# A low-rank conditioned feed-forward kernel in float32: factored adapters on 32x32 TensorE tiles, other DMA shapes, and an order by half tiles

## The chip, the cores and the metric

The kernel runs on one core of a Trainium2 chip. The metric is device time in microseconds (us) of one execution. The engines are named as the profile names them: PE is TensorE (PEld its weight loads), DVE is VectorE, ACT is ScalarE, POOL is GpSimd, SP is SyncE, which only issues transfers. Sixteen DMA engines move data between DRAM and the on-chip memory of 128 partitions (SBUF); PSUM is the memory into which PE accumulates.

## The reference

All data are float32. There are 8 batches of 512 tokens, rows of 2048 features. `itok` names one of 32 adapters for each batch; R is 16 and there are 8 experts.

```python
# y: a dense layer with a low-rank adapter per batch
base_out = einsum('bti,oi->bto', x, W) + b
lora_h   = einsum('bti,bir->btr', x, lora_As[itok])
y        = base_out + einsum('btr,bro->bto', lora_h, lora_Bs[itok]) * 2.0
# top-1 routed low-rank experts on y
logits = einsum('bsd,ed->bse', y, route_w)
topk_v, topk_idx = top_k(logits, 1)
h   = einsum('bsd,erd->bser', y, A)
wh  = (one_hot(topk_idx) * topk_v)[..., None] * h
out = x + einsum('bser,eor->bso', wh, Bw) * 1.0
```

Only 136 projections of y are needed, 128 for h (8 experts x 16) and 8 for the logits. With P the 2048x136 matrix of both, y P = x (W^T P) + b P + 2 (x A_b)(B_b P), so y itself is never formed.

## The kernel before, in words

**Fold.** P comes as `pj`: 16 chunks of 128 rows by 136. For each of 16 blocks of 128 rows of W (`load_w`, L101, 1 MB each, four buffers), ACT reorders the block into `wv` (L82) and PE accumulates W^T P into PSUM with 16 products (L189, `fold_w`). The result is `c_sb`, 2048x136. Beside this PE forms the bias part (`fold_bias`, L204), turns the gathered rows of the second adapter matrix (`turn_adapters`, L220), and multiplies them with P (`project_adapters`, L227) into `gm`, masked by batch. The adapters' rows come by two indirect transfers of POOL (L155, L162).

**Adapters.** `fold_adapters(b)` (L264) multiplies A of a batch with its part of `gm` and adds `c_sb`: a full matrix `m` of 2048x136 for each batch (L274 PE, L282 DVE). It is called for two batches at a time, so four times, in the order of `units`: two units of 256 tokens of a batch b, then two of batch b+4.

**Tokens.** A unit of 256 tokens is two tiles of 128. `load_x` brings a unit as [128 partitions, 8 groups of 32 tokens, 512 features]: partition quarter i holds features 512 i to 512 i + 511, and each partition of it one of 32 tokens. Four transfers do this, one for each quarter, two on SP's queue and two on ACT's (L115). `turn_x` (L296) turns a tile in 32x32 blocks on DVE, `heads` (L302) runs 16 products with `m` (each a float32 product of two instructions, L307) and then routes on DVE (L312 to L323); `turn_heads` (L334, L336) turns the weighted heads; `delta` (L339) runs 4 products for a quarter of the features (L343), turns them back on DVE (L345) and adds them to x on POOL (L350); `store` (L356) writes the unit in four transfers, two on SP's queue and two on POOL's. There are five buffers of x.

**Order.** The program is written out by hand (`manual_schedule`), and each engine runs its instructions in the order of the text. A loop over n interleaves heads of unit n with deltas of unit n-1 and the turn of unit n+1; the load of unit n+3 follows the store of unit n-1.

The views that shape the transfers before are these:

```python
        nc.sync.dma_start(out=wt, in_=w[ts(oc, P), :])
...
        return dram[b, ts(k, U), :].rearrange("(g t) (i d) -> i t g d", t=Q, i=NQ)
...
        for i, eng in ((0, nc.sync), (2, nc.scalar), (1, nc.sync), (3, nc.scalar)):
            eng.dma_start(out=xt[ts(i, Q)], in_=src[i])
```

Of the kernel before, what the change touches and what calls it, by code (L numbers as in the profile page):

```python
# [14 lines left out]
COND_SCALING = 2.0  # L15
# [3 lines left out]
def kernel(  # L19
# [28 lines left out]

    nc = tc.nc
# [15 lines left out]
    TPU = U // P  # L65
    NG = U // Q
    GJ = 4
    PH = P // 2
    HB = B // 2
    assert B * R == P and ER == P  # L70

    const = ctx.enter_context(tc.tile_pool(name="const", bufs=1))
    cpool = ctx.enter_context(tc.tile_pool(name="cpool", bufs=6))
    rpool = ctx.enter_context(tc.tile_pool(name="rpool", bufs=4))
    xpool = ctx.enter_context(tc.tile_pool(name="xpool", bufs=5))
    dpool = ctx.enter_context(tc.tile_pool(name="dpool", bufs=2))
    small = ctx.enter_context(tc.tile_pool(name="small", bufs=2))
    ps_s = ctx.enter_context(tc.tile_pool(name="ps_s", bufs=2, space=bass.MemoryType.PSUM))

    def chunked(copy, dst, src):  # L80

        copy(  # L82
            dst.rearrange("p j (i a) -> p j i a", a=Q),
            src.rearrange("p (i j a) -> p j i a", i=NQ, a=Q),
        )
# [6 lines left out]
    pj = cpool.tile([P, NO, NP], F32, tag="c", name="pj")  # L92
    proj_v = proj.rearrange("(c p) e -> p c e", p=P)
    bias_sb = const.tile([P, NO], F32, name="bias_sb")
    fb = const.tile([P, NJ, P], F32, name="fb")
# [3 lines left out]
    def load_w(oc):  # L99
        wt = rpool.tile([P, D], F32, tag="r", name=f"w_{oc}")  # L100
        nc.sync.dma_start(out=wt, in_=w[ts(oc, P), :])  # L101
        w_tiles.append(wt)

    units = [UPB * (b + h * HB) + k for b in range(HB) for h in range(2) for k in range(UPB)]
    x_tiles = {}

    def rows_of(dram, u):
        b, k = divmod(u, UPB)
        return dram[b, ts(k, U), :].rearrange("(g t) (i d) -> i t g d", t=Q, i=NQ)

    def load_x(u):
        xt = xpool.tile([P, NG, DQ], F32, tag="x", name=f"x_{u}")
        src = rows_of(x, u)
        for i, eng in ((0, nc.sync), (2, nc.scalar), (1, nc.sync), (3, nc.scalar)):
            eng.dma_start(out=xt[ts(i, Q)], in_=src[i])  # L115
        x_tiles[u] = xt

    nc.scalar.dma_start(out=pj[:, :2], in_=proj_v[:, :2])
    load_w(0)
    nc.scalar.dma_start(out=pj[:, 2:], in_=proj_v[:, 2:])  # L120
    nc.scalar.dma_start(out=bias_sb, in_=bias)
    for oc in range(1, 4):
        load_w(oc)
# [3 lines left out]
    make_identity(nc, ident)  # L127

    own_i = const.tile([P, B], I32, name="own_i")
    nc.gpsimd.iota(own_i, pattern=[[-R, B]], base=0, channel_multiplier=1)  # L130
    own = const.tile([P, B], F32, name="own")
# [6 lines left out]

    rank_i = const.tile([P, E], I32, name="rank_i")
    nc.gpsimd.iota(rank_i, pattern=[[-1, E]], base=E, channel_multiplier=0)  # L140
    rank = const.tile([P, E], F32, name="rank")
    nc.vector.tensor_copy(rank, rank_i)


    it_f = const.tile([P, B], F32, name="it_f")
    nc.vector.tensor_scalar(it_f, it_i, float(R), None, ALU.mult)
    nc.vector.tensor_tensor(it_f, it_f, own, ALU.add)
    nc.vector.tensor_tensor(it_f, it_f, mask, ALU.mult)
    row_f = const.tile([P, 1], F32, name="row_f")
    nc.vector.tensor_reduce(row_f, it_f, AX.X, ALU.add)  # L150
    row_i = const.tile([P, 1], I32, name="row_i")
    nc.vector.tensor_copy(row_i, row_f)
    raw = [xpool.tile([P, 2, D], F32, tag="x", name=f"raw_{k}") for k in range(2)]
    ad_b = raw[0][:, 0, :]
    nc.gpsimd.indirect_dma_start(  # L155
        out=ad_b,
        out_offset=None,
        in_=cond_b,
        in_offset=bass.IndirectOffsetOnAxis(ap=row_i, axis=0),
    )  # L160
    ad_ar = raw[0][:, 1, :]
    nc.gpsimd.indirect_dma_start(  # L162
        out=ad_ar,
        out_offset=None,
        in_=cond_a,
        in_offset=bass.IndirectOffsetOnAxis(ap=row_i, axis=0),
    )
    ad_a = const.tile([P, NJ, P], F32, name="ad_a")
    chunked(nc.gpsimd.tensor_copy, ad_a, ad_ar)


    c_sb = cpool.tile([P, NJ, NP], F32, tag="c", name="c_sb")
    GRP = 512 // NP
    groups = [(j0, min(GRP, NJ - j0)) for j0 in range(0, NJ, GRP)]
    c0b = const.tile([P, NP], F32, name="c0b")
    gm = const.tile([P, B, NP], F32, name="gm")

    with tc.tile_pool(name="ps_c", bufs=len(groups), space=bass.MemoryType.PSUM) as ps_c:
# [4 lines left out]
        def fold_w(oc):  # L183
            wv = dpool.tile([P, NJ, P], F32, tag="d", name=f"wv_{oc}")
            chunked(nc.scalar.copy, wv, w_tiles[oc])
            for pc, (j0, n) in zip(pcs, groups):
                for k in range(n):

                    nc.tensor.matmul(  # L189
                        pc[:, k, :],  # L190
                        wv[:, j0 + k, :],
                        pj[:, oc, :],
                        start=(oc == 0 and k == 0),
                        stop=(oc == NO - 1),
                        skip_group_check=True,
                    )
                if oc == NO - 1:
                    nc.scalar.copy(c_sb[:, j0 : j0 + n, :], pc[:, :n, :])

        def fold_bias():  # L200

            pb = ps_s.tile([1, NP], F32, tag="s", name="pb")
            for oc in range(NO):
                nc.tensor.matmul(  # L204
                    pb,
                    bias_sb[:, oc : oc + 1],
                    pj[:, oc, :],
                    start=(oc == 0),
                    stop=(oc == NO - 1),
                )  # L210
            c0 = const.tile([1, NP], F32, name="c0")
            nc.vector.tensor_copy(c0, pb)  # L212
            nc.gpsimd.partition_broadcast(c0b, c0)  # L213

        ad_bT = raw[1][:, 1, :].rearrange("p (c q) -> p c q", q=P)

        def turn_adapters(g):
            pt = ps_s.tile([P, 4, P], F32, tag="s", name=f"pbT_{g}")
            for k in range(4):
                nc.tensor.transpose(pt[:, k, :], ad_b[:, ts(4 * g + k, P)], ident)  # L220
            nc.scalar.copy(ad_bT[:, 4 * g : 4 * g + 4, :], pt)

        def project_adapters():

            pg = ps_s.tile([P, NP], F32, tag="s", name="pg")
            for oc in range(NO):
                nc.tensor.matmul(  # L227
                    pg,
                    ad_bT[:, oc, :],
                    pj[:, oc, :],  # L230
                    start=(oc == 0),
                    stop=(oc == NO - 1),
                )
            g_sb = const.tile([P, NP], F32, name="g_sb")
            nc.vector.tensor_copy(g_sb, pg)  # L235
            for b in range(B):
                nc.vector.tensor_scalar(
                    gm[:, b, :], g_sb, mask[:, b : b + 1], COND_SCALING, ALU.mult, ALU.mult
                )

        for oc in range(NO):
            fold_w(oc)
            if oc + 4 < NO:
                load_w(oc + 4)
            if oc == 2:
                fbr = raw[1][:, 0, :]
                nc.scalar.dma_start(out=fbr, in_=ffn_b)
                chunked(nc.gpsimd.tensor_copy, fb, fbr)
            if oc in (3, 6, 9):
                load_x(units[oc // 3 - 1])  # L250
            if oc == 7:
                fold_bias()
            if oc in (8, 9, 10, 11):
                turn_adapters(oc - 8)
            if oc == 12:
                project_adapters()
                load_x(units[3])
    ps_m = ctx.enter_context(tc.tile_pool(name="ps_m", bufs=2, space=bass.MemoryType.PSUM))
# [3 lines left out]
    m_tiles = {}  # L262

    def fold_adapters(b):  # L264
        pair = (b, b + HB)
        for bb in pair:
            m_tiles[bb] = cpool.tile([P, NJ, NP], F32, tag="c", name=f"m_{bb}")
        for j0, n in groups:
            pms = [
                ps_m.tile([P, GRP, NP], F32, tag="m", name=f"pm_{bb}_{j0}") for bb in pair  # L270
            ]
            for k in range(n):
                for h, bb in enumerate(pair):
                    nc.tensor.matmul(  # L274
                        pms[h][:, k, :],
                        ad_a[ts(h, PH), j0 + k, :],
                        gm[ts(h, PH), bb, :],
                        start=True,
                        stop=True,
                    )  # L280
            for h, bb in enumerate(pair):
                nc.vector.tensor_tensor(  # L282
                    m_tiles[bb][:, j0 : j0 + n, :],
                    c_sb[:, j0 : j0 + n, :],
                    pms[h][:, :n, :],
                    ALU.add,
                )


    xT_tiles = {}  # L290
    wh_tiles = {}
    whT_tiles = {}

    def turn_x(u, t):
        xT = rpool.tile([P, NJ, P], F32, tag="r", name=f"xT_{u}_{t}")
        nc.vector.transpose(  # L296
            xT.rearrange("p j (g t) -> p g j t", t=Q),
            x_tiles[u][:, ts(t, NQ), :].rearrange("p g (j a) -> p g j a", a=Q),
        )
        xT_tiles[u, t] = xT  # L300

    def heads(u, t):  # L302
        xT = xT_tiles.pop((u, t))
        m = m_tiles[u // UPB]
        ph = ps_s.tile([P, NP], F32, tag="s", name=f"ph_{u}_{t}")
        for j in range(NJ):
# [127 lines left out]
```

## Time and profile before

| | |
|---|---|
| time, median of 3 runs | 440.67 us (436.3 to 443.87) |
| time of the profiled execution | 436.82 us |
| its span, first to last instruction | 435.0 us |
| mean granted clock of TensorE | 0.915 of full |
| read from and written to DRAM | 54.60 MB and 33.55 MB, 203 GB/s over the span |

The profile's page has six parts: busy time of each engine; the span in 40 slices (a digit is a tenth; PEclk is the clock granted to TensorE, DMA the mean busy share of 16 DMA engines, GB/s what they moved); the DMA queues with packets, MB and share; the chain of waits followed back from the last instruction; the costliest groups of instructions as "line engine operation, out<-in, shapes, xcount | busy us, mean ns | idle before, and what ended it"; and the transfers as "out<-in, queue, xcount, KB each, median us from issue to landing". The queue q1 is SP's, q10 ACT's, q0 POOL's. A separate answer gives the same quantities for chosen stretches of time, and another the chain piece by piece in order of time.

In order of time, the first matmul starts at 21.6 us, the fold of W ends at about 105, the first heads run from about 120, and the last store is issued at 422.

### The profile page before, as it was taken

Reading aid. Unit: us, or ns where it says so; the run is one execution under the profiler, and the core shown is the slowest. Engines: PE = TensorE matmul, PEld = TensorE weight load, DVE = VectorE, ACT = ScalarE, POOL = GpSimd, SP = SyncE. Lnnn points to the kernel's source line nnn. Section 1 sums busy time; section 2 is a strip of 40 time slices with the busy share of each in tenths; the row PEclk is TensorE's granted clock in tenths of the full one; section 3 lists DMA queues with packets and bytes.
Section 4 is the critical chain, followed back from the end, with each engine's and each line's share of the span. In section 5 each row is a group of like instructions: output and inputs, shape, how many; then the busy total and the mean of one; then the engine's idle time right before and its main releaser. Section 6 shows DMA issues by size and latency. Waiting matters only on the chain.

```text
span 435.0 us, 5824 instructions
## 1 busy us (share of the span) xinstructions
PE 358.9 (83%) x2416; PEld 332.2 (76%) x2416; DVE 228.3 (52%) x388; ACT 42.1 (10%) x43; POOL 176.4 (41%) x110
## 2 busy tenths in 40 slices
PE   0099987598788996999999699999969999999900
PEld 0099866598687995999889599999858998999800
DVE  1000000010557886388787628888863887886620
ACT  0335332434000000000000000000000000000000
POOL 2111000000001764067675505867550585768780
PEclk9999999999579996799999759999976999999975
DMA  8999999991004099937999994599999459995596
GB/s 258 400 322 277 252 296 284 266 305 53 0 1 98 2 203 240 267 62 154 227 293 286 237 269 85 129 231 292 283 233 294 87 128 226 299 202 121 129 196 152
DMA packets 35738, 88.54 MB, mean 204 GB/s; under 512 B 2560, under 2 KB 4608, under 8 KB 33280
## 3 DMA queue, kind: packets, MB, share of 16 engines
q1 hardware_dynamic: 19712, 50.34, 43.7%
q10 hardware_dynamic: 11072, 18.95, 18.7%
q0 software_dynamic: 4928, 18.88, 15.5%
q8 instruction: 19, 0.31, 0.3%
q14 instruction: 7, 0.06, 0.0%
HBM read 54.60 MB, written 33.55 MB: 203 GB/s over the span
## 4 chain that ended last, share of the span: by engine, by line
PE 56%; DMA 12%; DVE 10%; POOL 7%; ACT 3%; issue 3%; ACTq 1%; POOLq 0%; SPq 0%; DVEq 0%
PE ph L307 20%; PE pd L343 15%; PE pc L189 10%; DMA out_dram<-x 9%; PE pm L274 8%; POOL x L350 7%; DMA x<-in_x_dram 3%; DVE m L282 3%; ACT wv L82 3%; DVE xT L296 3%; DVE dl L345 2%; PE pb L204 1%; PE pg L227 1%; ACTq L115 1%; POOL out_dram L356 1%
## 5 line engine op out<-in xcount | busy, mean ns | idle before, releaser
L350 POOL TENSOR_TENSOR x<-x,dl 128x1024 f32<-128x1024 f32 x64 | 149.6, 2360 | 189.4 <-DVE dl L345 187.0
L307 PE MATMUL ph<-m,xT 128*128 128x136 f32 x1024 | 131.9, 290 | 2.7 <-DVE xT L296 2.7
L307 PEld LDWEIGHTS ph<-m,xT 128*128 128x128 f32 x1024 | 129.8, 200 | 4.5 <-DVE xT L296 3.0
L343 PE MATMUL pd<-whT,fb 128*128 128x256 f32 x512 | 116.2, 380 | 3.6 <-ACT whT L336 3.6
L343 PEld LDWEIGHTS pd<-whT,fb 128*128 128x128 f32 x512 | 94.9, 190 | 16.6 <-ACT whT L336 4.9
L345 DVE STREAM_TRANSPOSE dl<-pd 128x1024 f32<-128x1024 f32 x64 | 80.0, 1250 | 24.1 <-PE pd L343 13.5
L189 PE MATMUL pc<-pj,wv 128*128 128x136 f32 x512 | 63.9, 287 | 32.4 <-ACT wv L82 32.4
L189 PEld LDWEIGHTS pc<-pj,wv 128*128 128x128 f32 x512 | 62.4, 196 | 33.8 <-ACT wv L82 33.6
L296 DVE STREAM_TRANSPOSE xT<-x 128x2048 f32<-128x2048 f32 x32 | 72.7, 2273 | 0.0
L274 PE MATMUL pm<-gm,ad_a 64*128 64x136 f32 x256 | 43.1, 416 | 14.2 <-DVE m L282 13.6
L274 PEld LDWEIGHTS pm<-gm,ad_a 64*128 64x128 f32 x256 | 35.3, 280 | 21.5 <-DVE m L282 20.2
L282 DVE TENSOR_TENSOR m<-c_sb,pm 128x408 f32<-128x408 f32 (+1 forms) x48 | 23.6, 526 | 34.1 <-PE pm L274 34.1
L336 ACT COPY whT<-pw 128x256 f32<-128x256 f32 x16 | 6.0, 373 | 295.0 <-PE pw L334 162.9
L82 ACT COPY wv<-w 128x2048 f32<-128x2048 f32 x16 | 30.3, 1899 | 29.3 <-PE pc L189 11.1
L312 DVE TENSOR_TENSOR hl<-ph,c0b 128x136 f32<-128x136 f32 x32 | 9.6, 299 | 32.2 <-PE ph L307 32.2
L212 DVE COPY c<-pb 1x136 f32<-1x136 f32 x1 | 0.3, 287 | 49.6 <-PE pb L204 49.6
L356 POOL DMA_DIRECT2D out_dram<-x x32 | 18.8, 592 | 4.8 <-POOL x L350 4.8
L235 DVE COPY g_sb<-pg 128x136 f32<-128x136 f32 x1 | 0.3, 300 | 34.9 <-PE pg L227 34.9
L213 POOL PARTITION_BROADCAST c0b<-c x1 | 0.5, 475 | 24.6 <-DVE c L212 24.6
L323 DVE TENSOR_TENSOR wh<-hl,rw 128x128 f32<-128x128 f32 x32 | 9.4, 293 | 1.1
L321 DVE TENSOR_SCALAR rw<-rank,win,top 128x8 f32<-128x8 f32 x32 | 9.3, 291 | 1.2
L334 PE MATMUL pw<-ident,wh 128*128 128x128 f32 x32 | 6.3, 274 | 2.1 <-DVE wh L323 2.1
(38 smaller groups left out, 63.4 us busy)
## 6 DMA issues: line engine op xcount, KB each, us to landing
w<-in_w_dram SPq DMA_DIRECT2D x16, 1024.0 KB, 16.1
x<-in_x_dram ACTq DMA_DIRECT2D x32, 512.0 KB, 8.8
x<-in_x_dram SPq DMA_DIRECT2D x32, 512.0 KB, 15.9
out_dram<-x SPq DMA_DIRECT2D x32, 512.0 KB, 9.0
out_dram<-x POOLq DMA_DIRECT2D x32, 512.0 KB, 10.9
raw<-in_ffn_b_dram ACTq DMA_DIRECT2D x1, 1024.0 KB, 4.8
pj<-in_proj_dram ACTq DMA_DIRECT2D x1, 952.0 KB, 22.2
pj<-in_proj_dram ACTq DMA_DIRECT2D x1, 136.0 KB, 9.0
```

Source lines behind the costliest of these rows:

```text
L82: copy(dst.rearrange("p j (i a) -> p j i a", a=Q), src.rearrange("p (i j a) -> p j i a", i=NQ, a=Q),)
L189: nc.tensor.matmul(pc[:, k, :], wv[:, j0 + k, :], pj[:, oc, :], start=(oc == 0 and k == 0), stop=(oc == NO - 1), skip_group_check=True,)
L274: nc.tensor.matmul(pms[h][:, k, :], ad_a[ts(h, PH), j0 + k, :], gm[ts(h, PH), bb, :], start=True, stop=True,)
L282: nc.vector.tensor_tensor(m_tiles[bb][:, j0 : j0 + n, :], c_sb[:, j0 : j0 + n, :], pms[h][:, :n, :], ALU.add,)
L296: nc.vector.transpose(xT.rearrange("p j (g t) -> p g j t", t=Q), x_tiles[u][:, ts(t, NQ), :].rearrange("p g (j a) -> p g j a", a=Q),)
L307: nc.tensor.matmul(ph, xT[:, j, :], m[:, j, :], start=(j == 0), stop=(j == NJ - 1))
L312: nc.vector.tensor_tensor(hl, ph, c0b, ALU.add)
L323: nc.vector.tensor_tensor(wh.rearrange("p (e r) -> p e r", r=R), hl[:, :ER].rearrange("p (e r) -> p e r", r=R), rw.unsqueeze(2).to_broadca ...
L343: nc.tensor.matmul(pd[:, k, :], fb[:, j0 + k, :], whT_tiles[u], start=True, stop=True)
L345: nc.vector.transpose(dl.rearrange("p g (k a) -> p k g a", a=Q), pd.rearrange("p k (g t) -> p k g t", t=Q),)
L350: nc.gpsimd.tensor_tensor(xs, xs, dl, ALU.add)
L356: eng.dma_start(out=dst[i], in_=xt[ts(i, Q)])
```

## The change

Adapters: no matrix per batch is formed. `cm` holds the folded W once, 136 columns, with 16 columns on either side for the adapter matrix A of an even and of an odd batch. `heads` multiplies x with 152 of these columns, so that PE forms x A_b beside x W^T P. `turn_low` copies the 16 numbers of each token to SBUF and turns them in 32x32 blocks; `add_low` multiplies each quarter of 32 tokens, on a diagonal 32x32 tile of PE, with `g4`, which holds the small matrix of the batch and the bias on each quarter of partitions, and adds to the same PSUM sums. `spread_adapters` makes `g4`. ACT copies the next batch's A into `cm`.

Fold: W, proj and the adapters are laid out by features i, j, a (i a quarter of 512 features, j one of 16 chunks, a one of 32), so that DVE's block turns replace PE's transposes; the copies into `wv` are halved between ACT and DVE; the bias product moves to DVE; the gathers become eight.

Transfers: x and out move in eight transfers of a unit, one for each group of 32 tokens, over 128 partitions; W in 16 and proj in 16 transfers over 128 partitions, with the views below. All of these are issued by SP. The order of the units is that of the batches.

Order: a loop over half tiles writes for each step half of a tile's heads, one quarter of a delta, the turn of half a tile, and the previous quarter's turn back and add.

```diff
-        wt = rpool.tile([P, D], F32, tag="r", name=f"w_{oc}")
-        nc.sync.dma_start(out=wt, in_=w[ts(oc, P), :])
+    proj_v = proj.rearrange("(i j a) e -> j i a e", i=NQ, a=Q)
+    w_v = w.rearrange("(i j a) d -> j i a d", i=NQ, a=Q)
+    def load_pj(j):
+        nc.sync.dma_start(out=pj[:, j, :], in_=proj_v[j])
+        nc.sync.dma_start(out=wt, in_=w_v[j])
...
     def rows_of(dram, u):
         b, k = divmod(u, UPB)
-        return dram[b, ts(k, U), :].rearrange("(g t) (i d) -> i t g d", t=Q, i=NQ)
+        return dram[b, ts(k, U), :].rearrange("(g t) (i d) -> g i t d", t=Q, i=NQ)
     def load_x(u):
         xt = xpool.tile([P, NG, DQ], F32, tag="x", name=f"x_{u}")
         src = rows_of(x, u)
-        for i, eng in ((0, nc.sync), (2, nc.scalar), (1, nc.sync), (3, nc.scalar)):
-            eng.dma_start(out=xt[ts(i, Q)], in_=src[i])
+        for g in range(NG):
+            nc.sync.dma_start(out=xt[:, g, :], in_=src[g])
...
+        def gather(v, table):
+            for m in range(NQ):
+                nc.gpsimd.indirect_dma_start(
...
+        gather(ad_br, cond_b)
+        gather(ad_ar, cond_a)
+        nc.gpsimd.dma_start(out=bias_o, in_=bias)
+        nc.gpsimd.dma_start(out=fbr, in_=ffn_b)
...
-            chunked(nc.scalar.copy, wv, w_tiles[oc])
+            chunked(nc.scalar.copy, wv, w_tiles[oc], 0)
+            chunked(nc.vector.tensor_copy, wv, w_tiles[oc], 1)
...
+        def turn_bias():
+            for i in range(NQ):
+                for k in range(NQ):
+                    nc.gpsimd.tensor_copy(
...
+        def fold_bias(js):
+            for j in js:
...
+                    nc.vector.scalar_tensor_tensor(
+                        bp, pj[:, j, :], bias_q[:, j : j + 1], bp, ALU.mult, ALU.add
+                    )
...
+        def spread_adapters(b0):
+            n = min(GRP, B - b0)
+            pq = ps_s.tile([P, GRP, NP], F32, tag="s", name=f"pq_{b0}")
+            nc.tensor.matmul(
+                pq[:, :n, :],
+                sel.rearrange("p i s -> p (i s)"),
+                gm[:, b0 : b0 + n, :],
+                start=True,
+                stop=True,
+            )
+            nc.vector.tensor_tensor(
+                g4[:, b0 : b0 + n, :],
+                pq[:, :n, :],
+                c0q.unsqueeze(1).to_broadcast([P, n, NP]),
+                ALU.add,
+            )
...
-    def fold_adapters(b):
...
+        for j in range(h * HJ, (h + 1) * HJ):
             nc.tensor.matmul(
-                ph, xT[:, j, :], m[:, j, :], start=(j == 0), stop=(j == NJ - 1)
+                ph_tiles[t],
+                xT_tiles[t][:, j, :],
+                cm[:, j, ds(s * R, NA)],
+                start=(j == 0),
+                stop=(j == NJ - 1),
             )
+    def turn_low(t):
+        s = batch_of(t) % 2
+        nc.scalar.copy(hls[t % 2][:, :R], ph_tiles[t][:, ds(s * NP, R)])
+        hT = small.tile([P, Q], F32, tag="hT", name=f"hT_{t}")
+        nc.vector.transpose(hT, hls[t % 2])
+        hT_tiles[t] = hT
+    def add_low(t):
+        b = batch_of(t)
+        s = b % 2
+        hT = hT_tiles.pop(t)
+        for i in range(NQ):
+            nc.tensor.matmul(
+                ph_tiles[t][ts(i, Q), ds((1 - s) * R, NP)],
+                hT[ts(i, Q), :],
+                g4[ts(i, Q), b, :],
+                start=False,
+                stop=True,
+                skip_group_check=True,
+                tile_position=(i * Q, i * Q),
+            )
...
+    def add_delta(u, q):
...
+        nc.gpsimd.tensor_tensor(xs, xs, dl, ALU.add)
+        if q == NQ - 1:
+            xt = x_tiles.pop(u)
+            dst = rows_of(out, u)
+            for g in range(NG):
+                nc.sync.dma_start(out=dst[g], in_=xt[:, g, :])
+            if u + 5 < NU:
+                load_x(u + 5)
...
+    for n in range(2 * NT + 2 * TPU + 1):
+        t, h = divmod(n, 2)
+        if t < NT:
+            heads(t, h)
+        if h == 0 and 0 < t <= NT:
+            route(t - 1)
+        if piece(n - 1):
+            add_delta(*piece(n - 1))
+        turn_x(t + 1, h)
+        if piece(n):
+            delta(*piece(n))
+        if h == 0 and 0 < t <= NT:
+            turn_heads(t - 1)
+        if h == 1 and t < NT:
+            turn_low(t)
+            add_low(t)
+            b, k = divmod(t, TPU * UPB)
+            if k == 0 and 0 < b < B - 1:
+                nc.scalar.copy(
+                    cm[:, :, ds((b + 1) % 2 * NA, R)], ad_aT[:, :, ts(b + 1, R)]
+                )
```

## The prediction, made before the changed kernel was run

> **What bounds the kernel now.** I read the page's span and slices first, then the chain of waits, then the groups, then stretches of the DMA rows.
>
> ```profile
> span 435.0 us, 5824 instructions
> PE 358.9 (83%) x2416; PEld 332.2 (76%) x2416; DVE 228.3 (52%) x388; ACT 42.1 (10%) x43; POOL 176.4 (41%) x110
> DMA  8999999991004099937999994599999459995596
> GB/s 258 400 322 277 252 296 284 266 305 53 0 1 98 2 203 240 267 62 154 227 293 286 237 269 85 129 231 292 283 233 294 87 128 226 299 202 121 129 196 152
> PE 56%; DMA 12%; DVE 10%; POOL 7%; ACT 3%; issue 3%; ACTq 1%; POOLq 0%; SPq 0%; DVEq 0%
> ```
>
> TensorE sets the end for 56% of the span and the transfers for 12%, but the DMA digits are 9 in more than half of the slices: the transfers are nearly a second bound. The chain inside a batch, in order of time, shows the pace of TensorE:
>
> ```profile
> 260.24 3.45 PE pd L343 x16
> 263.70 3.71 PE ph L307 x32
> 267.40 3.45 PE pd L343 x16
> 271.07 3.71 PE ph L307 x32
> ```
>
> So a unit of 256 tokens costs 2 x (3.71 + 3.45) = 14.3 us of TensorE plus 0.4 us of small transposes. It moves 2.1 MB in and 2.1 MB out. At 435 us nothing else matters as long as the 88.5 MB move near 300 GB/s, so the question that I put to the change is: how many of the 16 DMA engines does each transfer run on, and how fast is one? The page answers the first for the kernel before.
>
> ```profile
> q1 hardware_dynamic: 19712, 50.34, 43.7%
> q10 hardware_dynamic: 11072, 18.95, 18.7%
> w<-in_w_dram SPq DMA_DIRECT2D x16, 1024.0 KB, 16.1
> x<-in_x_dram SPq DMA_DIRECT2D x32, 512.0 KB, 15.9
> out_dram<-x SPq DMA_DIRECT2D x32, 512.0 KB, 9.0
> ```
>
> Queue q1 is SP's. Its x and out rows are 64 x 256 rows of 2 KB = 16384 packets, its W rows 16 x 128 of 8 KB = 2048. 19712 - 18432 = 1280 = 80 transfers x 16: one closing packet for each engine that took part. So all 80 run on 16 engines (q10 gives the same: 10496 rows + 36 x 16 = 11072). The speed of one engine, from the table of stretches:
>
> ```profile
> core 0: us, PE busy (x) PEld busy (x) DVE busy (x) ACT busy (x) POOL busy (x), PEclk, DMA share, GB/s
> 8.00:20.00 12.00, 0.00 (x0) 0.00 (x0) 0.82 (x5) 1.62 (x2) 2.05 (x2) 1.00 1.02 416
> 136.00:138.00 2.00, 2.00 (x15) 1.90 (x14) 0.75 (x4) 0.00 (x0) 0.00 (x0) 1.00 1.01 204
> 162.00:164.00 2.00, 1.38 (x16) 0.93 (x14) 1.63 (x2) 0.00 (x0) 2.00 (x1) 1.00 1.04 283
> 423.00:427.00 4.00, 0.00 (x0) 0.00 (x0) 0.00 (x0) 0.00 (x0) 0.00 (x0) 0.50 0.93 189
> ```
>
> W alone, 128 partitions and 8 KB rows: 416/16 = 26 GB/s per engine. x loads alone, 32 partitions and 2 KB rows: 204/16/1.01 = 12.6. Stores alone: 189/16/0.93 = 12.7. Loads and stores mixed: 283/16/1.04 = 17. A 2 KB packet thus costs between 79 ns (at 26 GB/s) and 162 ns (at 12.6), and 120 ns when mixed. The trace does not say whether 162 comes from 2 KB or from 16 engines meeting in 32 partitions.
>
> **The change, transfers first.** The new views put a dimension of 4 outermost on the DRAM side: `g i t d` for x and out (i=4, t=32, 2 KB rows), `j i a d` for W and `j i a e` for proj. The quarters don't merge with the rows inside them, since their steps differ. Before, `i t g d` was indexed by i, so that t=32 was outermost, and W had 128.
>
> The row says 16 engines for every transfer of the kernel before, outer size 32 or 128. The Trainium skill (DMA: Bandwidth & Descriptors, section "Why a DMA increments its semaphore by 16 and not by 1", under "How many engines") says that a transfer is split along the slowest dimension of each side, over the largest count up to 16 that divides both; the page's rule table adds that an outer size under 16 confines it to that many engines. 128 on the SBUF side and 4 on the DRAM side give 4 engines. It agrees with the rows here (32 and 128 give 16), but no row here has an outer size of 4. By the row (16 engines go on) the transfers fit under TensorE, rival C. By the rule 12 engines sit idle. The rule covers just the case that the trace lacks, so I take it.
>
> Work per engine, four engines, all of it on SP's one queue:
> - x and out: 67.1 MB in 2 KB rows = 32768 packets, 8192 per engine. At 79 ns 647 us, at 162 ns 1327 us. Four engines now meet in four different quarters of the partitions, which speaks for the low end; 2 KB rows, and quarters walked in step, speak for the high one. I take the mixed row, 120 ns: **983 us**.
> - W: 16.8 MB over 4 x 26 GB/s = **161 us** (twice that if the slow row's halving holds for 8 KB rows too, which no row shows).
> - proj: 16 x 32 packets of 544 B per engine, 21 ns by bytes to 79 ns as a whole small packet: 11 to 40, **26 us**.
> - Gaps: SP issues store u, then stands at the load of u+5, which reuses that buffer and waits for the store to land; queued behind it is the store of u+1. 11 such turns. The landing tail is about 1.5 us (4.1 us the quickest 512 KB of x, less 2.6 at 200 GB/s) and the issue about 0.4: **22 us**; nothing if the wait is cut by row group.
> - First issue (0.7) and the end after the last byte (432 to 435): **5 us**.
>
> Sum: 983 + 161 + 26 + 22 + 5 = 1197 us span; the profiled time before is 436.82 for a span of 435.0, so **1199 us**. The median shown, 440.67, is 0.9% above that profiled run; that is small here.
>
> **The edits that I cost at nothing**, because a unit now waits for 1024 rows of load and 1024 of store, 2048 / 4 = 512 packets per engine, 512 x 120 ns = 61 us of transfer (40 at 79 ns). The rows from which their work is sized:
>
> ```profile
> L307 PE MATMUL ph<-m,xT 128*128 128x136 f32 x1024 | 131.9, 290 | 2.7 <-DVE xT L296 2.7
> L343 PE MATMUL pd<-whT,fb 128*128 128x256 f32 x512 | 116.2, 380 | 3.6 <-ACT whT L336 3.6
> L274 PE MATMUL pm<-gm,ad_a 64*128 64x136 f32 x256 | 43.1, 416 | 14.2 <-DVE m L282 13.6
> L350 POOL TENSOR_TENSOR x<-x,dl 128x1024 f32<-128x1024 f32 x64 | 149.6, 2360 | 189.4 <-DVE dl L345 187.0
> L345 DVE STREAM_TRANSPOSE dl<-pd 128x1024 f32<-128x1024 f32 x64 | 80.0, 1250 | 24.1 <-PE pd L343 13.5
> ```
>
> - TensorE, per tile of 128 tokens: head matmuls grow from 136 to 152 columns, 3.71 x 152/136 = 4.15 us; delta 3.45; transpose 0.19; the diagonal tiles, 4 matmuls in 2 passes = 8 instructions, no such row: from 2 x 0.116 (four at once) to 8 x 0.116 = 0.93 (in line; 0.116 = 3.71/32), I take the middle, 0.6. Together 8.4, a unit 16.8 us. The 256 pm instructions (43.1 us and their 13.6 of waits), the bias sum and 16 transposes go; three spreads and one bias matmul come (some 2 us).
> - DVE, per tile: turns 2.27 in two halves, deltas 2 x 1.25, routing 1.1 (the 0.30 add and one 0.17 multiply go), one small turn 0.2: 6.1. In the fold it takes half of each W copy, 0.6 to 1.2 us against ACT's 1.90 for a whole one, and 16 bias steps of 0.3.
> - POOL: 4 x 2.36 per unit as before; 32 store issues of 0.59 go; 6 more gathers of 1.0, two loads and 16 tiny copies (0.1 to 0.2 each) come, early and beside W.
> - ACT: half copies, 32 of hl and 16 more of whT at 0.3; its 32 load issues go. SP: 288 issues instead of 80 at 0.3 to 1.1 us (its issue rows), 90 to 310 us spread under 1200.
>
> If that cover were gone a unit would cost 16.8, not 61. One rule cuts here: the Trainium skill (TensorE: Matmul & The Clock Gate, Part 1) has the array at half clock after a few us idle; the stretch 423 to 427 shows 0.50. A unit at full clock is 16.8, at half 34: under 40 and 61 both, so the sum is the same by either. What is late next: x of u+5, hence turn, heads and all behind them; nothing computes its way past that.
>
> **Rivals.**
> - A: four engines at the free 79 ns. For it: their targets are 128 partitions, as W's at 26 GB/s. Against: 2 KB rows, never seen above 17. 647 + 161 + 11 + 5 = 824, with gaps **850**.
> - B: four engines, slow packets: 1327 + 161 to 322 + 40 + 22 + 5, 1555 to 1716, **1600**. For it: the two rows at 12.6. Against: there 16 engines crowd 32 partitions.
> - C, the other side: the transfers stay on 16 engines. Then TensorE decides: first W at 8 us instead of 20, 16 folds of 3.97, 5 for what surrounds them, 32 x 8.4, and about 25 for the last unit's deltas and stores and the odd wait: 8 + 64 + 5 + 269 + 25 + 13 for a late x now and then = **384 us**, faster. The point from which it decides: a unit's 4.2 MB under 16.8 us, 250 GB/s, which takes ten engines at 26.
> - The change not doing what it says (the diagonals giving no gain) changes only C, by under 20 us.
>
> **How the numbers follow.** Middle case (packets of 100 to 145 ns, 1030 to 1400 us): 0.45, and its own working is the predicted 1199. A (to 1030): 0.27. B (from 1400): 0.19. C: 0.08; within 2%: 0.01. So faster 0.08, same 0.01, slower 0.91; 2% is about what a measurement of this kernel tells from no change. The range 850 to 1600 leaves out C, the lower edge of A and the upper third of B, 0.2 in all.
>
> **What would show it.** Right: DMA digits near 2 in every slice (4 of 16 engines), 55 to 100 GB/s; SP's queue with 32768 + 2048 + 2048 rows + 288 x 4 = 38016 packets (x 16 would be 41472); the chain nearly all DMA x and out; PEclk 5 in most slices; w landing in tens of us; TensorE busy little changed. The share of one engine per packet separates A, the middle and B. Wrong: 41472 packets, or GB/s above 110: then C.

## The result, and the profile after

The changed kernel takes 900.11 us (median; 892.43 to 919.63), against 440.78 us for the kernel before: 2.043 times as long (95% interval 2.018 to 2.069). The forecast was slower, 1199 us in a range of 850 to 1600. The profiled execution took 892.43 us.

The page after, its parts in the order in which they were shown of before: span, engines, granted clock, DMA and GB/s by slices, SP's queue, the chain.

```profile
span 890.7 us, 6058 instructions
PE 388.9 (44%) x2376; PEld 349.7 (39%) x2376; DVE 218.7 (25%) x393; ACT 36.4 (4%) x94; POOL 165.9 (19%) x102
PEclk9767867667799978686857676868585858587555
DMA  2622222222222222222222222222222222222222
GB/s 64 191 92 104 104 103 104 102 104 103 104 102 102 101 88 100 89 102 92 98 86 100 89 102 91 102 91 102 91 101 92 98 85 102 90 102 103 102 102 95
q1 hardware_dynamic: 38016, 85.00, 24.9%
SPq 62%; DMA 24%; PE 2%; issue 2%; POOL 1%; DVE 1%; POOLq 0%; ACT 0%; ACTq 0%; DVEq 0%
```

The DMA digits are 2 from the third slice to the last, where before they were mostly 9: four engines of sixteen. The 6 in the second slice is the gathers and ffn_b on POOL's queue, which do spread. From the fourth slice on, the rate stands at 100 to 104 GB/s with dips to 85. SP's queue has 38016 packets, which is 36864 rows + 288 x 4: the 288 transfers closed on four engines each. TensorE went from 56% of the chain to 2%. In its place stands SP's own queue: in the loop most issues of a store take 2.5 to 4.5 us, where those of before took 0.4 (median). This fits an SP that stands behind transfers still under way, since after each pause its first issues take 0.5 to 0.7 us again.

Two stretches of the loop show what became of TensorE (columns as in the prediction's table): ten units with their gaps, and one gap.

```profile
290.00:730.00 440.00, 199.54 (x1231) 175.50 (x1229) 124.08 (x211) 11.17 (x49) 101.13 (x43) 0.73 0.25 95
324.00:340.00 16.00, 2.05 (x14) 1.64 (x15) 4.76 (x10) 0.00 (x0) 2.35 (x1) 0.51 0.26 101
```

TensorE is busy for less than half of the time, and its granted clock falls to 0.51 where it stands idle, while the four DMA engines stay full (a share of 0.25 is four of sixteen).

### The profile page after: what moved, and what is told of

The parts are those of the page before. It is cut to its first block, busy times and chain, and to the rows that moved or that the text cites. A ratio compares the mean times of both kernels' runs of the same rounds, so it can differ in the third digit from the quotient of the medians.

```text
span 890.7 us, 6058 instructions
## 1 busy us (share of the span) xinstructions
PE 388.9 (44%) x2376; PEld 349.7 (39%) x2376; DVE 218.7 (25%) x393; ACT 36.4 (4%) x94; POOL 165.9 (19%) x102
## 2 busy tenths in 40 slices
DMA packets 38891, 88.53 MB, mean 99 GB/s; under 512 B 1344, under 2 KB 3408, under 8 KB 36688
## 3 DMA queue, kind: packets, MB, share of 16 engines
q1 hardware_dynamic: 38016, 85.00, 24.9%
## 4 chain that ended last, share of the span: by engine, by line
SPq 62%; DMA 24%; PE 2%; issue 2%; POOL 1%; DVE 1%; POOLq 0%; ACT 0%; ACTq 0%; DVEq 0%
SPq L121 29%; SPq L459 23%; DMA out_dram<-x 17%; SPq L97 6%; DMA w<-in_w_dram 6%; SPq L91 4%; DMA x<-in_x_dram 1%; PE ph L378 1%; POOL x L454 1%; PE pd L441 1%; DVE dl L449 0%; POOLq L538 0%; ACT wv L231 0%; PE ph L399 0%; DVE xT L224 0%
## 5 line engine op out<-in xcount | busy, mean ns | idle before, releaser
L378 PE MATMUL ph<-cm,xT 128*128 128x152 f32 x1024 | 165.0, 321 | 1.8 <-DVE xT L224 1.8
L378 PEld LDWEIGHTS ph<-cm,xT 128*128 128x128 f32 x1024 | 153.5, 212 | 13.1 <-issue 10.9
L224 DVE STREAM_TRANSPOSE xT<-x 128x1024 f32<-128x1024 f32 x64 | 77.6, 1219 | 329.2 <-DMA x<-in_x_dram 329.2
L248 PE MATMUL pc<-pj,wv 128*128 128x136 f32 x512 | 93.6, 363 | 144.5 <-ACT wv L231 116.0
L248 PEld LDWEIGHTS pc<-pj,wv 128*128 128x128 f32 x512 | 90.3, 267 | 148.6 <-ACT wv L231 119.8
L399 PE MATMUL ph<-g,hT 32*32 32x136 f32 x256 | 16.6, 335 | 273.6 <-DVE hT L391 273.6
L231 DVE COPY wv<-w 128x1024 f32<-128x1024 f32 x16 | 11.0, 693 | 145.0 <-DMA w<-in_w_dram 145.0
L435 ACT COPY whT<-pw 128x128 f32<-128x128 f32 x32 | 8.5, 266 | 480.1 <-PE pw L432 480.1
L231 ACT COPY wv<-w 128x1024 f32<-128x1024 f32 x16 | 16.7, 1046 | 205.9 <-DMA w<-in_w_dram 205.9
L421 DVE TENSOR_TENSOR wh<-ph,rw 128x128 f32<-128x128 f32 x32 | 9.3, 292 | 1.1
```

Source lines behind the costliest of these rows:

```text
L224: nc.vector.transpose(dst[:, ts(h, HJ), :].rearrange("p j (g t) -> p g j t", t=Q), src.rearrange("p g (j a) -> p g j a", a=Q)[:, :, ts(h, ...
L231: copy(dst[:, ts(h, HJ), :].rearrange("p j (i a) -> p j i a", a=Q), src.rearrange("p (i j a) -> p j i a", i=NQ, a=Q)[:, ts(h, HJ)],)
L248: nc.tensor.matmul(pc[:, k, :], wv[:, j0 + k, :], pj[:, oc, :], start=(oc == 0 and k == 0), stop=(oc == NO - 1), skip_group_check=True,)
L378: nc.tensor.matmul(ph_tiles[t], xT_tiles[t][:, j, :], cm[:, j, ds(s * R, NA)], start=(j == 0), stop=(j == NJ - 1),)
L399: nc.tensor.matmul(ph_tiles[t][ts(i, Q), ds((1 - s) * R, NP)], hT[ts(i, Q), :], g4[ts(i, Q), b, :], start=False, stop=True, skip_group_che ...
```

## The experiments

The theory: the outer dimension of 4 puts every transfer of SP on the same four engines, at 80 ns for a packet of 2 KB. The rivals: one SP queue for everything is slow whatever the shape of its transfers; the new arithmetic or order is to blame; packets in quarters are slow in themselves.

**e1_rates: the transfers alone.** Nothing is computed: x is copied to out through SBUF by this, for six shapes in turn:

```diff
+        for k in range(n):
+            for a, d in pieces(how, x, tl[:, k], u + k):
+                eng.dma_start(out=a, in_=d)
+        for k in range(n):
+            for a, d in pieces(how, out, tl[:, k], u + k):
+                eng.dma_start(out=d, in_=a)
```

> Transfers alone: x is copied to out with no computation (the second term of the reference is left out). Six stretches, each loads and then stores units of 256 tokens in 2 KB rows: (1) 128 partitions, DRAM outer size 128, SP; (2) quarters of 32 partitions as in the kernel before, SP; (3) the changed kernel's view, 128 partitions with an outer 4, SP; (4) 8 partitions at a time, outer 8, SP; (5) as 3 but issued by POOL; (6) 64 partitions with an outer 2, one unit. Theory 'engine count': the DMA share is 1.0, 1.0, 0.25, 0.5, more than 0.25, 0.125, and (3) runs at 102 GB/s as in the changed kernel, (6) at 51. Rival 'one queue': a single SP queue is slow whatever the shape, so (1), (2) and (3) are alike. Second question, the 2 KB packet: if 2 KB alone costs 160 ns, (1) gives 200 GB/s; if crowding in few partitions does, (1) gives about 400, (2) 200, and (4), 8 engines in 8 partitions, falls under 102 instead of reaching 204.

Ten stretches of its trace (columns: length, POOL's issuing, granted clock, DMA share, GB/s). The sixth may begin with the last loads of its shape, and the last holds loads and stores; every 5 us of either reads the same rate.

```profile
core 0: us, POOL busy (x), PEclk, DMA share, GB/s
10.00:20.00 10.00, 0.00 (x0) 1.00 1.05 389
25.00:35.00 10.00, 0.00 (x0) 1.00 1.06 388
45.00:60.00 15.00, 0.00 (x0) 1.00 1.07 222
72.00:80.00 8.00, 0.00 (x0) 1.00 1.05 397
90.00:130.00 40.00, 0.00 (x0) 1.00 0.26 102
140.00:200.00 60.00, 0.00 (x0) 1.00 0.26 102
220.00:300.00 80.00, 0.00 (x0) 1.00 0.54 62
330.00:360.00 30.00, 0.00 (x0) 1.00 0.48 103
380.00:395.00 15.00, 8.12 (x12) 1.00 1.06 213
455.00:530.00 75.00, 0.00 (x0) 1.00 0.13 51
q1 hardware_dynamic: 28800, 54.53, 38.6%
```

In pairs, load then store: (1) 128 partitions on 16 engines, 389 and 388; (2) quarters, 222 and 397; (3) the changed kernel's view, 102 and 102 at a share of 0.26; (4) eighths, 62 and 103. Then (5) the load by POOL, 213 at a share of 1.06, and (6) the outer 2, 51 at 0.13. All of (1) to (4) and (6) went through the one SP queue, so the queue is not slow. Nor is the size of a transfer to blame: (1) and (3) both move pieces of 256 KB between DRAM and 128 partitions. The engine count fits: 2 engines 51, 4 engines 102, 16 engines 389. So do the packets of SP's queue: 28800 is 26624 rows + 48 x 16 + 24 x 16 + 48 x 4 + 96 x 8 + 32 x 2, the transfers of each shape times the engines that its outer size allows. The second question is answered too: 2 KB rows are not slow in themselves, and loads halve when they land in 32 partitions; in 8 partitions eight engines are slower than four in 128. Stores out of few partitions lose less, and from quarters nothing here.

**e2_xout16 and e3_all16: undo the views.** In e2 x and out go in quarters again, on SP alone; in e3 W and proj go in quarters too. The stores and proj, left out here, are changed in the same way.

```diff
-        return dram[b, ts(k, U), :].rearrange("(g t) (i d) -> g i t d", t=Q, i=NQ)
+        return dram[b, ts(k, U), :].rearrange("(g t) (i d) -> i t g d", t=Q, i=NQ)
-        for g in range(NG):
-            nc.sync.dma_start(out=xt[:, g, :], in_=src[g])
+        for i in (0, 2, 1, 3):
+            nc.sync.dma_start(out=xt[ts(i, Q)], in_=src[i])
...
-        nc.sync.dma_start(out=wt, in_=w_v[j])
+        for i in range(NQ):
+            nc.sync.dma_start(out=wt[ts(i, Q)], in_=w_v[j, i])
```

> The changed kernel with x and out moved in quarters of 32 partitions as before (outer size 32), all still on SP's one queue; W and proj keep the outer 4. Engine count: W and proj still take about 175 us at 102 GB/s, a unit then 4.2 MB at 200 GB/s plus 3.5 us of gap = 24.5 us, in all about 535 us, with TensorE still not the bound. One queue: about 890, unchanged.

> As the run before it, and W and proj in quarters of 32 partitions too, all on SP's queue: nothing is left on 4 engines, all the rest of the change stays. Engine count: the fold ends near 100 us, the loop at 24.5 us a unit while loads go on, in all 420 to 450 us, so about the kernel before. One queue: about 890.

Measured: e2 524.9 us, ratio to the kernel before 1.207 (1.189 to 1.225); e3 413.2 us, 0.952 (0.942 to 0.961). With no transfer of SP left on four engines, the changed kernel is faster than the one before: the four runs of e3, at most 416.0 us, lie below all seven of the kernel before on the same chip (431.82 to 439.48). In ratios, x and out cost 2.043 - 1.207 = 0.836 (some 368 us) and W with proj 0.256 (some 112 us). "One queue" and "the new arithmetic or order" both fall: e3 keeps both. A stretch of e2's loop, then three of e3 (columns as in the prediction's table), show where the time goes:

```profile
260.00:460.00 200.00, 200.00 (x1382) 177.03 (x1381) 144.43 (x244) 12.33 (x54) 113.23 (x49) 1.00 0.82 218
20.00:60.00 40.00, 26.76 (x181) 25.82 (x180) 7.62 (x9) 6.28 (x6) 8.29 (x23) 0.83 1.02 236
60.00:100.00 40.00, 20.71 (x155) 19.70 (x154) 9.95 (x22) 5.23 (x5) 0.00 (x0) 0.81 1.00 213
200.00:280.00 80.00, 80.00 (x553) 70.55 (x552) 57.31 (x99) 4.70 (x21) 45.06 (x20) 1.00 0.91 244
```

In both loops TensorE is busy all the time: it is the bound again. Here both expectations missed. They had TensorE wait for 24.5 us of transfers a unit, and e3 came out below its 420 to 450 us. The transfers kept up at 218 to 244 GB/s, above the 200 that was taken. From the first head product to the last, e2 and e3 take 254.5 us each, against 551.6 in the changed kernel; what W with proj cost lies ahead of that, where the first head runs at 126.9 us in e3 and at 241.8 in e2. From 20 to 100, in the fold, e3's TensorE is busy for 47 of 80 and all 16 engines are full at 213 to 236 GB/s, about e1's rate for loads in quarters.

**e4_before_wide: the view of x and out, in the kernel before.** As in the changed kernel, SP alone issues them.

```diff
-        return dram[b, ts(k, U), :].rearrange("(g t) (i d) -> i t g d", t=Q, i=NQ)
+        return dram[b, ts(k, U), :].rearrange("(g t) (i d) -> g i t d", t=Q, i=NQ)
-        for i, eng in ((0, nc.sync), (2, nc.scalar), (1, nc.sync), (3, nc.scalar)):
-            eng.dma_start(out=xt[ts(i, Q)], in_=src[i])
+        for g in range(NG):
+            nc.sync.dma_start(out=xt[:, g, :], in_=src[g])
...
-        for i, eng in ((0, nc.sync), (2, nc.gpsimd), (1, nc.sync), (3, nc.gpsimd)):
-            eng.dma_start(out=dst[i], in_=xt[ts(i, Q)])
+        for g in range(NG):
+            nc.sync.dma_start(out=dst[g], in_=xt[:, g, :])
```

> The kernel before with one edit: x and out in eight transfers of a unit over 128 partitions with the outer 4, on SP. Engine count: 67.1 MB at 102 GB/s = 658 us, beside W's 45 to 60 at 16 engines, and gaps of 3.5 us at 12 units: 740 to 790 us; W's stretch stays above 300 GB/s. If the rest of the change were to blame for the slowdown: near 440.

Measured: 774.13 us in one run (436.58 for the kernel before on the same chip). W at the start, the loop, and SP's queue:

```profile
0.00:20.00 20.00, 0.00 (x0) 0.00 (x0) 1.49 (x10) 1.43 (x2) 3.81 (x11) 1.00 0.93 328
200.00:700.00 500.00, 250.93 (x1453) 229.96 (x1453) 174.35 (x294) 4.47 (x12) 119.17 (x52) 0.72 0.26 102
q1 hardware_dynamic: 36096, 83.89, 29.4%
```

W, whose view still has 128 outermost, keeps 328 GB/s at the start; the loop runs at the share 0.26 and 102 GB/s. The queue's packets are 34816 rows + 256 x 4 + 16 x 16: in one and the same queue, x and out close on four engines and W on sixteen. The view of x and out brings this slowdown with no other part of the change but SP as the only issuer, and e1 and e3 show that SP alone is not slow.

**e6_gap: the wait of SP for its own store.** Each reload is written one store later.

```diff
-            if u + 5 < NU:
-                load_x(u + 5)
+            if u and u + 4 < NU:
+                load_x(u + 4)
```

> The changed kernel with each reload of an x buffer written one store later (unit u+4 after the store of unit u), so that the store it waits for has landed; all transfers keep their 4 engines. Gap theory: the page's 11 turns stand with idle engines for about 2.7 us each, so 30 us go: 855 to 870 us. If the wait of SP is hidden by what is still queued: 885 to 900. No expectation reaches below 840, since 67.1 MB at 102 GB/s stay.

Measured: 859.56 us, ratio 1.957 (1.946 to 1.969). SP's longest waits in the changed kernel, and then in e6:

```profile
SPq L121 <- DMA out_dram<-x: 122.1, 44, 3.7
SPq L538 <- DMA out_dram<-x: 10.6, 5, 2.5
SPq L97 <- ACT wv L231: 2.7, 2, 1.4
...
```

```profile
SPq L538 <- DMA out_dram<-x: 10.3, 5, 2.5
SPq L97 <- ACT wv L231: 2.6, 2, 1.3
SPq L459 <- POOL x L454: 0.9, 1, 0.9
...
```

A stretch of e6's loop, to be set beside the 95 GB/s of the changed kernel's:

```profile
300.00:700.00 400.00, 183.39 (x1121) 161.30 (x1120) 114.25 (x196) 9.86 (x43) 91.62 (x40) 0.72 0.26 102
```

The load's wait for the store (L121) is gone, the rate no longer dips, and 33 us of span are gone with it (890.7 to 857.4). By difference, the other 89 of those 122 us were spent by SP while the engines still worked off what was queued. So a wait of a queue is worth what the engines stand idle, and here that is 3 us a turn.

**e7_pool_store: the same view, other engines.**

```diff
-                nc.sync.dma_start(out=dst[g], in_=xt[:, g, :])
+                nc.gpsimd.dma_start(out=dst[g], in_=xt[:, g, :])
```

> The changed kernel with the stores issued by POOL instead of SP, same view (outer 4); loads, W and proj unchanged. In e1 the same view issued by POOL moved 213 GB/s at a DMA share of 1.06[...]. If the cost in the changed kernel is that every transfer falls on the same four engines, those keep the loads and a quarter of the stores, 2.6 MB of a unit's 4.2 at 102 GB/s = 26 us instead of 43.7, and the kernel takes 600 to 680 us with DMA digits of 4 to 6. If it is four engines whichever they are, or the stores are not to blame: 870 to 910.

Measured: 674.3 and 693.66 us in two runs, one inside and one just above what was expected. The DMA digits of the slower one:

```profile
DMA  2542222222222222676463644736263563744555
```

They rise from 2 to between 2 and 7 as soon as stores begin. So the same small outer dimension costs less when POOL issues the stores, and more than four engines are then at work. That POOL's transfers take other engines in turn is an inference: the trace names no engine. POOL's queue also cuts its transfers in another way (27456 packets under 512 B on e7's page, 1344 on the changed kernel's), so e7 does not single out the choice of engines. That it is still slow fits the loads, which stay on SP's four, but also e1, where POOL's stores ran unevenly, at 65 to 192 GB/s in slices of 5 us from 405 to 445 us; neither was tried apart.

**e5_fold16 and e8_pw_pieces: the change without its views, and the fold as before.** W comes in blocks of 128 contiguous rows again, with a copy of proj in that order; a second copy in quarters serves the adapters; x and out go in quarters on SP, as in e2. In e8 the first copy of proj comes in pieces on SP's queue.

```diff
-        nc.sync.dma_start(out=wt, in_=w_v[j])
+        nc.sync.dma_start(out=wt, in_=w[ts(j, P), :])
...
+    nc.scalar.dma_start(out=pw_[:, :2], in_=projw_v[:, :2])
...
+    nc.scalar.dma_start(out=pw_[:, 2:], in_=projw_v[:, 2:])
```

> The changed kernel with nothing on 4 engines and W not in quarters either: W in blocks of 128 contiguous rows (DRAM outer 128) with proj in the same order by ACT's queue as before; a second copy of proj in quarters for the adapters and the bias; x and out in quarters on SP. In e3 the fold ended near 125 us because W came in quarters of 32 partitions at 213 GB/s. If that is the cause, W now comes at 400, the fold ends at 85 to 95 us bound by TensorE, and the loop, TensorE-bound at 8.2 us a tile, is unchanged: 375 to 388 us. If the fold was late for another reason (proj in small rows, the copies of W on two engines), 405 to 413.

> As e5, but the copy of proj for W's fold comes in 16 pieces on SP's queue, each just ahead of the block of W that needs it (128 rows of 544 B, DRAM outer 128), where e5 brought it in two pieces on ACT's queue and the page shows TensorE waiting 26 us for the second. If that wait delays the fold and the fold sets the start of the loop: 12 to 20 us less than e5, 367 to 375 us. If the loop's start is set by the bytes that lie before the first x (the transfers are at a share of 0.92 to 1.04 from 0 to 90 us in e5): 382 to 390, as e5.

Measured: e5 386.86 us, ratio 0.881 (0.877 to 0.885), faster than both kernels. The four runs of e8 lie between 384.15 and 393.72 us, those of e5 between 386.06 and 390.95: no gain that could be told, and none near the 367 to 375 of the first expectation. The work of one tile in e5's loop, from the chain:

```profile
208.62 2.07 PE ph L375 x16
210.69 1.73 PE pd L438 x8
212.41 0.36 PE ph L396 x8
212.78 2.27 PE ph L375 x16
215.04 1.73 PE pd L438 x8
216.77 0.11 PE pw L429
```

That is 8.27 us for 128 tokens, with no piece of anything but TensorE in it. Of the time before the loop, these lines are TensorE's longest wait in e5, its longest in e8, and 20 to 60 us of e8:

```profile
PE pc L245 <- DMA pw__77<-in_proj_dram: 26.0, 2, 16.0
PE pc L243 <- ACT wv L226: 24.1, 7, 7.3
20.00:60.00 40.00, 34.10 (x260) 33.32 (x261) 16.17 (x28) 8.38 (x8) 5.63 (x19) 0.91 1.06 326
```

In e8 the wait for proj is gone, a wait for the copies of W stands in its place, and the transfers are at a share of 1.06. The first head product runs at 104.6 us in e5 and at 105.3 in e8. In the chain it is reached by a load of x in e5 and by one of W in e8. So the start of the loop goes by the bytes that are moved before it, as the second expectation had it, though the last of them need not be x.

## Why the prediction was right, step by step

The mechanism was right: twelve of sixteen engines fell idle, and the transfers set the time. The size was not: 1199 us lies a third above 900.11. The result is where the prediction put rival A (to 1030 us, chance 0.27), not its own middle case, and it lies in the range because the range reached down to A.

- **Sixteen engines before, four after.** Right, to the packet: 38016 against 38016 forecast. The rule on the slowest dimension (the Trainium skill, DMA: Bandwidth & Descriptors, "How many engines") held for 2, 4, 8 and 16 on SP, by the packets of e1 and e4.
- **The price of a packet.** This term was mis-sized. 120 ns was taken between 79 and 162; 102 GB/s on four engines is 25.5 each, 2048 / 25.5 = 80 ns, the low end. The row of W, divided by its share like the other three, had shown just that: 416 / 16 / 1.02 = 25.5. With it x and out take 8192 x 80.3 ns = 658 us instead of 983, a difference of 325, larger than the whole miss of 307 us (1199 against 892.43). The fault lay in how the end was chosen: the mixed row's 17 GB/s came from the same quarters as the slow rows, so it was no witness for engines that don't meet in one quarter. The Trainium skill has a rule that spoke for the low end (SBUF — State Buffer, "Door 1: The DMA port swizzle"): the rate goes by how many of 16 ports the partitions reach, and partitions 0 to 31 reach half, with 189 GB/s measured there. By it the 12.6 GB/s an engine would be crowding, and 128 partitions reach all ports; of four engines that walk four quarters in step it says nothing. e1 agrees for loads: 222 in quarters, 389 in 128 partitions. Its stores from quarters, 397, do not show the halving.
- **W:** 161 us forecast; 16.8 MB at the 104 GB/s of its slices is 161.
- **Gaps:** 22 us forecast, 33 by e6's span. The place was right; each of the 11 turns costs nearer 3 us than 2.
- **proj:** 26 us forecast within 11 to 40. What is left of the span, 890.7 - 658 - 161 - 33 - 5 = 34 us, bounds it from above if the other terms hold; it was not measured by itself.
- **The edits costed at nothing.** Right: the chain gives TensorE 2%. From 290 to 730 us, ten units of 43.7 us, it was busy for 199.5 us, 19.8 a unit, at a mean granted clock of 0.73. It did slow down between units, to 0.51, as the clock rule in the prediction said, and stayed under the cover of 41 us of transfer (4.2 MB at 102 GB/s).
- **Signs that did not come.** The digits of the granted clock run from 5 to 9, where 5 was forecast for most slices: within a unit's work the clock came back to 1.00 (from 344 to 360 us, after 0.50 from 328 to 340). The rate stood at the top of the forecast 55 to 100 GB/s: 99 over the span, 102 in most of the loop. The chain names SP's issues of x and out (62% with W's) before the transfers themselves (24%).
- **Rival A** (850) was the nearest, **B** fell with e1, and the price that **C** put on the change without its transfers, 384 us, is near e5's 386.86, in part by luck: e5 moves W and x another way, its loop begins at 104.6 us where C has 77, and 18 us follow its last matmul where C has 25 and 13. Inside it: a tile 8.4 us forecast, 8.27 measured. Half of a tile's heads takes 2.07 us, as forecast (4.15 for both), but the half behind the diagonal products 2.27; with these 0.20 the four products cost 0.36 + 0.20 = 0.56 us, against 0.6 forecast.

## What to carry to other kernels

Before judging a transfer by the partitions it fills, read the outermost size on each side of it, the DRAM side too: on SP's queue a `rearrange` that puts a 4 in front took twelve of sixteen engines away, and the packet count of the queue tells it in one subtraction. When two rows bound a cost, ask what else the slow row differs in before taking the middle. And a change that loses as a whole can hold a gain: here the arithmetic and the order are worth 12% once x, out and W have the shapes of before.

## What the runs showed of the hardware that was not expected

- Eight engines loading into 8 partitions move 62 GB/s, less than four engines into 128 partitions (102), at a DMA share of 0.54: the share tells how many engines are busy, not how fast they move.
- Loads in quarters run at 222 GB/s, stores from quarters at 397 in e1, where twelve of them are queued. The kernel before drained its last stores at 189, with SP's and POOL's queues both at work. In e3, with SP alone, the last unit's stores begin at 193 to 207 and rise to 332 within seven us, so the second queue is not needed for the low rate. What sets it, these runs do not tell.
- The same view with an outer 4 gave 102 GB/s issued by SP and 213 issued by POOL, at a share of 1.06.
- The four diagonal 32x32 products overlap: in e5's trace they run as two passes of four instructions; the four start within 20 ns of each other, the passes 120 ns apart, where a 136-column instruction in line takes 116. But the way to small tiles and back shows. The first of them starts 0.31 us after the last delta instruction, where 0.22 is usual, and the two head instructions behind them start 0.21 and 0.23 us after the one before, where 0.13 is usual. What holds them up was not tried.
